# A gated recurrent layer on one core: the products with the state in three banks of 128 columns

## The chip, the core and the metric

The kernel runs on one NeuronCore of a Trainium2 chip. Five engines work beside each other, each through its own instructions in order: TensorE (PE, with the weight loads shown as a row of their own, PEld), VectorE (DVE), ScalarE (ACT), GpSimd (POOL) and SyncE (SP, which issues the DMAs). They meet at semaphores. [...] The metric is the device time of one execution in microseconds; the kernel before takes 1627.62 us in the median of three runs (1627.06 to 1628.18).

## The reference

Eight sequences of 512 steps, 512 features wide, go through one recurrent layer with a gate `r` on the hidden product and an output gate `z`, and the input is added to the result. With `h` the state (8 x 512, float32):

```
fused  = sigmoid([x_t, h] @ w_W + w_b)            # 512+512 wide
r, z   = split(fused)
memory = x_t @ wx_W + wx_b + r * (h @ wh_W + wh_b)
h_new  = z * h + (1 - z) * tanh(memory)
out_t  = x_t + h_new
```

Everything with `x_t` alone can be computed ahead, for many steps at once. The three products with `h` (`r`, `z` and `hh = h @ wh_W`, 512 x 512 each) can't: they stand in a chain of 512 steps.

## The kernel before

**Layout.** The 512 features are cut into four pieces of 128 (`k`, 0 to 3, on the partitions as rows of the contraction) and the 512 outputs into four quarters (`j`) of 32 partitions. Of the outputs there are two halves: half A is what contraction pieces 0 and 1 of the next step need, half B what pieces 2 and 3 need. So `z` of half A is 64 columns on 128 partitions, and likewise `r`, `hh` and half B: six blocks of 64 columns a step.

**The products with the state** (lines 535 to 552). For a piece `k` the state (128 x 32: four steps of eight sequences, of which one step counts) is loaded as the weights, and the columns of the weight matrices stream through. Each product is four matmuls, one for each quarter `j`, which run side by side in the array, and each float32 matmul stands in the trace as two. A *group* here means four such matmuls beside each other: a product of one `k` with one bank is two groups, eight matmul records. `ORDER` says in which order `(bank, k)` come:

- bank A, `k` 0 and 1: 256 columns: the part of `hh` of half B, `hh`, `z` and `r` of half A
- bank A, `k` 2 and 3: 192 columns (without `hh` of half B)
- bank D, `k` 0 to 3: 128 columns, `z` and `r` of half B
- bank H, `k` 2 and 3: 64 columns, the rest of `hh` of half B

`hh` of half B so lies in two pieces, in banks A and H. PSUM is filled ahead with the input's part and the bias (`spread`, ScalarE), four steps at a time, and the two sets of banks alternate every four steps. Behind the state's products of a step come products of the input for later chunks (`deal`, into the banks `xp`), three units of 96 columns in most steps and four in one of sixteen; the last sixteen steps have none. DVE drains them (`drain`, line 431), SP moves halves across partitions and POOL adds up (`result`).

**After the products.** Features must get back onto partitions, so each block is turned by a 32 x 32 transpose on VectorE. VectorE's order in a step is written out by hand (lines 654 to 683): turn `r` of A (`tr`, line 577); turn `hh` of A (`md1A`, 592); turn `z` of A (`tz`, 577); a mark (`settle`, 600: a one-element memset that waits until an earlier transpose has finished writing, since VectorE does not wait for its own results); two scans `m` of half A (`memory`, 565); turn the first part of `hh` of B (`md1B`, 636); turn `r` of B (`tr<-D`); the first update of half A (`update`, 565: a scan `hT<-hd0A`); turn the second part of `hh` of B (592); the second update of A; a mark; two scans `m` of B; two transposes of `z` of B (`hd0B`, 629); a mark (632); two updates of B (`hT<-hd0B`). Then come whatever drains and transposes of the input's part fall due (`turn_x`), and two idle memsets (710). The scans multiply and add along short chains: `m` of B has three terms, of A two.

ScalarE's order is the sigmoid of `r` of A, the sigmoid of `z` of A (both from turned SBUF tiles), two tanh of A, two sigmoids for `r` of B, the sigmoid of `z` of B straight from bank D, two tanh of B, two copies of the new state. Then come the copies of `spread`.

Pieces 0 and 1 of the next step wait for the updates of half A, pieces 2 and 3 for those of half B.

Of the kernel before, what the change touches and what calls it, by code (L numbers as in the profile page):

```python
# [7 lines left out]
F32 = mybir.dt.float32  # L8
BF16 = mybir.dt.bfloat16
AF = mybir.ActivationFunctionType  # L10
# [3 lines left out]
P = 128  # L14
NQ = 4
GS = 4
B = 8
HU = 64
# [3 lines left out]
DVE_FILL = 23  # L22
IDLE = 5
# [34 lines left out]
AHEAD = (  # L58
    (((), ""), ((0,), "AD"), ((1, 2, 3), "H")),
    (((0,), "A"), ((1,), "D"), ((2, 3), "H")),  # L60
    (((0,), "A"), ((1, 2, 3), "D"), ((), "H")),
    (((0,), "A"), ((1, 2), "D"), ((3,), "H")),
)
# [6 lines left out]

SC = slice(128, 512)

XP = {"A": slice(0, 256), "X": slice(256, 384), "D": slice(384, 512), "H": slice(512, 576)}


@with_exitstack
def tile_cond_rnn_residual(
# [111 lines left out]
    nc.scalar.activation(const.tile([P, 1], F32, name="table"), zeros[:, :1], AF.Sigmoid)  # L189
    for n, t_ in enumerate(hd0[0] + hd0[1] + md0[0] + md0[1] + hT[0] + hT[1] + md1[1]):  # L190
        (nc.vector if n < DVE_FILL else nc.gpsimd).memset(t_, 0.0)
    for t_ in md0[1]:
        nc.gpsimd.memset(t_[:, :, :, 1], 1.0)
    for t_ in hd0[0] + hd0[1]:
# [10 lines left out]
    tt = const.tile([P, 7 * BL], F32, name="tt")  # L205
    xs = [const.tile([P, 576], F32, name=f"xs{n}") for n in range(4)]

# [15 lines left out]

    for t_ in xps + [whole[1]["H"], whole[1]["A"]] + list(banks[0].values()):
        mm(t_, none, none[:, :1].broadcast_to([P, t_.shape[1]]), start=True)
    for n in range(2):
        mm(whole[1]["D"], zeros[:, :128], zeros, start=n == 0)

    def bank_of(g):

        return {2: whole[1]["H"], 3: whole[1]["A"], 4: whole[1]["D"]}.get(g, xps[g % 2])

# [24 lines left out]
    for t_ in off:  # L257
        nc.gpsimd.memset(t_, 0.0)
    for t_ in xs:
        nc.gpsimd.memset(t_[:, :64], 0.0)  # L260
    for t_ in xs[1:] + xs[:1]:
        nc.gpsimd.tensor_copy(t_[:, 64:128], bias[:, :64])
        nc.gpsimd.tensor_copy(t_[:, 512:], bias[:, 448:])
    c0 = COLS.start
# [41 lines left out]
    def source(g, c0, c1):  # L306

        return xs[g % GS][:, c0:c1] if g else xps[0][:, c0 - 64 : c1 - 64]

    def spread(g, names):  # L310

        for n in names:
            skip = 64 if n == "A" and not g else 0
            nc.scalar.copy(banks[g % 2][n][:, skip:], source(g, XP[n].start + skip, XP[n].stop))

    def turn_x(g, e):

        c0 = XP["X"].start + 32 * e
        nc.vector.transpose(md1[e // 2][g % 2][:, :, e % 2, 1 + e // 2], source(g, c0, c0 + 32))

# [158 lines left out]
    for n in (2, 1, 3):  # L479
        weight_sum(n, slice(0, 1))  # L480
    spread(0, "HDA")
    keep(1)
# [41 lines left out]
    for i in range(T):  # L524
# [10 lines left out]
        for n in (ORDER if i else FIRST).split():  # L535
            if n == "x":
                take(first[1], 1)
                if k_ == 0:
                    keep(2)
                k_ += 1  # L540
                continue
            bank, k = n[0], int(n[1])
            hs = hT[k // 2][i % NH][:, :, k % 2, 2]
            to, w_ = {
                "A": (ps["A"], wa) if k < 2 else (ps["A"][:, 64:], wa[:, :, :, 64:]),
                "D": (ps["D"], wd),
                "H": (ps["H"], wa[:, :, :, :64]),
            }[bank]
            if bank == "A" and i == 0:
                to, w_ = xps[0][:, :HALF], wa[:, :, :, 64:]  # L550
            for j in range(NQ):
                mm(to[32 * j : 32 * j + 32, :], hs, w_[:, k, j])
# [18 lines left out]

        pa = ps["A"][:, HU:] if i else xps[0][:, :HALF]
        raw = {"h": (pa[:, :HU], ps["H"]), "z": (pa[:, HU : 2 * HU],), "r": (pa[:, 2 * HU :], ps["D"][:, HU:])}

        def turned(n, hf):
            t_ = work.tile([P, 2, 32], F32, tag=f"t{n}{hf}", name=f"t{n}{hf}_{i}")
            inst = nc.vector.transpose(t_.rearrange("p c n -> p (c n)"), raw[n][hf]).ins  # L577
            return t_[:, :, rows], inst

        h_done = [None, None]  # L580

        def turn_r():
            tr, _ = turned("r", 0)
            act(
                ("r", 0, g % 2, s),
                md0[0][g % 2][:, rows, :, 1].rearrange("p n c -> p c n"),
                tr,
                AF.Sigmoid,
            )

        def turn_h(hf):
            inst = nc.vector.transpose(  # L592
                md1[hf][g % 2][:, :, :, hf].rearrange("p n c -> p c n"), raw["h"][hf]
            ).ins
            h_done[hf] = inst
# [3 lines left out]
        def settle(hf):  # L599
            inst = nc.vector.memset(idle[:, IDLE - 2 + hf : IDLE - 1 + hf], 0.0).ins  # L600
            tc.add_manual_dep(inst, h_done[hf].name, SYNC)

        def turn_z():
            tz, _ = turned("z", 0)
            settle(0)
            act(
                ("zc", i % 2),
                hd0[0][i % 2][:, :, :, 2].rearrange("p n c -> p c n"),
                tz,
                AF.Sigmoid,  # L610
                scale=-1.0,
            )

        def turn_r_b():
            t_, _ = turned("r", 1)
            for q in range(2):
                act(
                    ("r", 1, q, g % 2, s),
                    md0[1][g % 2][:, rows, q : q + 1, 2].rearrange("p n c -> p c n"),
                    t_[:, q : q + 1],  # L620
                    AF.Sigmoid,
                )
            sz = work.tile([P, HU], F32, tag="sz", name=f"sz_{i}")
            act(("sz", i % 4), sz, ps["D"][:, :HU], AF.Sigmoid, scale=-1.0)
            return sz

        def turn_sz(sz):
            done = [
                nc.vector.transpose(hd0[1][i % 2][:, :, q, 2], sz[:, 32 * q : 32 * q + 32]).ins  # L629
                for q in range(2)  # L630
            ]
            mark = nc.vector.memset(idle[:, IDLE - 3 : IDLE - 2], 0.0).ins
            tc.add_manual_dep(mark, done[0].name, SYNC)

        def turn_part():
            nc.vector.transpose(md1[1][g % 2][:, :, :, 0].rearrange("p n c -> p c n"), ps["A"][:, :HU])  # L636

        ms = [
            work.tile([P, 2, B, 2 + hf], F32, tag=f"m{hf}", name=f"m{hf}_{i}").rearrange("p c n s -> p n c s")
            for hf in range(2)  # L640
        ]

        def memory(hf, q):

            c_ = slice(q, q + 1)
            scan(c_, ms[hf], md0[hf][g % 2][:, rows], md1[hf][g % 2][:, rows])
            act(("n", hf, q, i % NH), state(hf, i, 1)[:, :, c_], ms[hf][:, :, c_, 1 + hf], AF.Tanh)

        def update(hf, q):
            new = hT[hf][(i + 1) % NH][:, B * s1 : B * s1 + B]  # L650
            z_ = hd0[hf][i % 2][:, rows] if hf else hd0[hf][i % 2]
            return scan(slice(q, q + 1), new, z_, hT[hf][i % NH][:, rows])
# [12 lines left out]
        update(0, 0)  # L665
        turn_h(1)
        update(0, 1)
        settle(1)
        if i == 0:

# [9 lines left out]
        memory(1, 1)  # L680
        turn_sz(sz)
        update(1, 0)
# [10 lines left out]
        if i < 3:  # L693
            spread(1, "HDA"[i])
            turn_x(1, i)
# [11 lines left out]
        for w in late.get(i, ()):  # L707
            inner_weight(*w)
        for n in range(IDLE - 3):
            nc.vector.memset(idle[:, n : n + 1], 0.0)  # L710
# [104 lines left out]
```

## Time and profile before

| | |
|---|---|
| median of three runs | 1627.62 us (1627.06 to 1628.18) |
| span of the profiled execution, first to last instruction | 1625.9 us |
| TensorE matmul rows busy | 1616.3 us (99%) |
| TensorE weight loads busy | 1308.3 us (80%) |
| VectorE busy | 1411.1 us (87%) |
| ScalarE busy | 1023.8 us (63%) |
| GpSimd busy | 539.1 us (33%) |
| granted TensorE clock | 1.000 over the span |

The span is that of the profiled execution alone; the runs' median is 1.7 us above it. Busy times of PE overlap (a matmul's record goes from its start to its modelled end, and the next has long begun), so 99% says that PE always had something in flight, not that it could not be fed faster. How long a stage takes is read from the chain of waits, which cuts PE's time without overlap, and from the starts of the rows in the timeline. One step is some 3.1 us.

### The profile page before, as it was taken

Reading aid. Unit: us, or ns where it says so; the run is one execution under the profiler, and the core shown is the slowest. Engines: PE = TensorE matmul, PEld = TensorE weight load, DVE = VectorE, ACT = ScalarE, POOL = GpSimd, SP = SyncE. Lnnn points to the kernel's source line nnn. Section 1 sums busy time; section 2 is a strip of 40 time slices with the busy share of each in tenths; the row PEclk is TensorE's granted clock in tenths of the full one; section 3 lists DMA queues with packets and bytes.
Section 4 is the critical chain, followed back from the end, with each engine's and each line's share of the span. In section 5 each row is a group of like instructions: output and inputs, shape, how many; then the busy total and the mean of one; then the engine's idle time right before and its main releaser. Section 6 shows DMA issues by size and latency. Waiting matters only on the chain.

```text
span 1625.9 us, 120027 instructions
## 1 busy us (share of the span) xinstructions
PE 1616.3 (99%) x49211; PEld 1308.3 (80%) x49211; DVE 1411.1 (87%) x11757; ACT 1023.8 (63%) x6033; POOL 539.1 (33%) x1443
## 2 busy tenths in 40 slices
PE   9999999999999999999999999999999999999998
PEld 5888888888888888888888888888888888888876
DVE  8988888888888888888888888888888888888887
ACT  4666666666666666666666666666666666666665
POOL 2323333333333333333333333333333333333321
PEclk9999999999999999999999999999999999999999
DMA  4011111111111111111111111111111111110110
GB/s 192 12 40 33 29 37 38 43 32 33 31 43 39 35 34 31 39 38 39 33 29 37 38 43 32 30 35 43 38 33 34 32 39 38 39 34 25 31 35 10
DMA packets 66217, 62.04 MB, mean 38 GB/s; under 512 B 9856, under 2 KB 64000, under 8 KB 65664
## 3 DMA queue, kind: packets, MB, share of 16 engines
q1 hardware_dynamic: 65664, 54.35, 12.7%
q8 instruction: 385, 6.31, 1.7%
q14 instruction: 168, 1.38, 0.3%
HBM read 14.96 MB, written 8.39 MB: 14 GB/s over the span
## 4 chain that ended last, share of the span: by engine, by line
PE 98%; DVE 1%; issue 0%; ACT 0%; DVEq 0%
PE A L219 49%; PE D L219 27%; PE xp L219 16%; PE H L219 7%; DVE tr L577 0%; DVE m L565 0%; DVE md1B L636 0%; DVE hT L565 0%; DVE md1A L592 0%; DVE tz L577 0%; DVE zeros L185 0%; DVE hd0B L629 0%; DVE md1B L592 0%; DVE idle L600 0%; ACT hT L285 0%
## 5 line engine op out<-in xcount | busy, mean ns | idle before, releaser
L219 PE MATMUL A<-wa,hT 128*32 128x256 f32 x16352 | 877.8, 355 | 4.2 <-DVE hT L565 4.2
L219 PEld LDWEIGHTS A<-wa,hT 128*32 128x32 f32 x16352 | 497.5, 123 | 260.2 <-DVE hT L565 135.6
L219 PE MATMUL D<-wd,hT 128*32 128x128 f32 x16384 | 541.0, 273 | 0.0
L219 PEld LDWEIGHTS D<-wd,hT 128*32 128x32 f32 x16384 | 480.4, 122 | 21.8 <-DMA wd<-in_wd_dram 0.5
L731 POOL TENSOR_TENSOR ot<-xin,hT 128x32 f32<-128x32 f32 x503 | 134.4, 267 | 1046.5 <-DVE hT L565 1028.8
L285 ACT ACTIVATE md0A<-tr 128x16 f32<-128x16 f32 x512 | 112.9, 221 | 385.2 <-DVE tr L577 385.2
L285 ACT ACTIVATE hT<-m 128x8 f32<-128x8 f32 x2048 | 324.2, 207 | 46.8 <-DVE m L565 0.4
L577 DVE STREAM_TRANSPOSE tr<-A 128x64 f32<-128x64 f32 x511 | 127.8, 250 | 199.4 <-PE A L219 198.2
L285 ACT ACTIVATE hT<-hT 128x16 f32<-128x16 f32 x1024 | 232.3, 227 | 91.4 <-DVE hT L565 89.9
L219 PE MATMUL H<-wa,hT 128*32 128x64 f32 x8208 | 208.3, 219 | 0.0
L285 ACT ACTIVATE md0B<-tr 128x8 f32<-128x8 f32 x1024 | 160.0, 206 | 42.6 <-DVE tr L577 1.2
L219 PEld LDWEIGHTS H<-wa,hT 128*32 128x32 f32 x8208 | 185.6, 122 | 0.0
L565 DVE TENSOR_TENSOR_SCAN hT<-hd0B,hT 128x24 f32<-128x24 f32 x1024 | 171.4, 208 | 0.8 <-DVE hT L565 0.8
L565 DVE TENSOR_TENSOR_SCAN hT<-hd0A,hT 128x24 f32<-128x24 f32 x1024 | 171.9, 168 | 0.0
L565 DVE TENSOR_TENSOR_SCAN m<-md0B,md1B 128x24 f32<-128x24 f32 x1024 | 154.5, 193 | 0.5 <-issue 0.4
L629 DVE STREAM_TRANSPOSE hd0B<-sz 128x32 f32<-128x32 f32 x1024 | 148.5, 190 | 0.0
L565 DVE TENSOR_TENSOR_SCAN m<-md0A,md1A 128x16 f32<-128x16 f32 x1024 | 142.5, 181 | 5.1
L219 PE MATMUL xp<-ti,si 128*32 128x192 f32 (+1 forms) x3120 | 146.7, 295 | 0.0
L450 POOL TENSOR_TENSOR xs<-ff 128x192 f32<-128x192 f32 x240 | 139.5, 597 | 0.1
L636 DVE STREAM_TRANSPOSE md1B<-A 128x64 f32<-128x64 f32 x511 | 130.1, 255 | 0.0
L285 ACT ACTIVATE hd0A<-tz 128x16 f32<-128x16 f32 x512 | 116.6, 228 | 21.2
L592 DVE STREAM_TRANSPOSE md1B<-H 128x64 f32<-128x64 f32 x512 | 128.3, 251 | 0.0
(110 smaller groups left out, 1861.0 us busy)
## 6 DMA issues: line engine op xcount, KB each, us to landing
ff<-tt SPq DMA_DIRECT2D x120, 96.0 KB, 2.6
ff<-tt SPq DMA_DIRECT2D x120, 72.0 KB, 2.2
out_dram<-ot SPq DMA_DIRECT2D x128, 64.0 KB, 1.8
xin<-in_x_dram SPq DMA_DIRECT2D x112, 64.0 KB, 2.1
ff<-ff SPq DMA_DIRECT2D x60, 96.0 KB, 2.1
ff<-ff SPq DMA_DIRECT2D x60, 72.0 KB, 2.7
wx<-in_wx_dram SPq DMA_DIRECT2D x4, 768.0 KB, 7.3
wa<-in_wa_dram SPq DMA_DIRECT2D x4, 512.0 KB, 11.1
```

What stands on the lines that cost most here:

```text
L219: nc.tensor.matmul(out_, lhsT, rhs, start=start, stop=False, skip_group_check=True)
L285: inst = nc.scalar.activation(out_, in_, func, **kw).ins
L450: nc.gpsimd.tensor_tensor(to, a, b, ALU.add)
L565: return nc.vector.tensor_tensor_scan(*[t_[:, :, c_].rearrange("p n c s -> p (n c s)") for t_ in (out_, d0, d1)], 0.0, ALU.mult, ALU.add,).ins
L577: inst = nc.vector.transpose(t_.rearrange("p c n -> p (c n)"), raw[n][hf]).ins
L592: inst = nc.vector.transpose(md1[hf][g % 2][:, :, :, hf].rearrange("p n c -> p c n"), raw["h"][hf]).ins
L629: nc.vector.transpose(hd0[1][i % 2][:, :, q, 2], sz[:, 32 * q : 32 * q + 32]).ins
L636: nc.vector.transpose(md1[1][g % 2][:, :, :, 0].rearrange("p n c -> p c n"), ps["A"][:, :HU])
L731: pool_done[i + 1] = nc.gpsimd.tensor_tensor(ot[:, t], x_of(c, slice(0, NQ), t, 1), hTs[(i + 1) % NH][:, :, :, B * s1 : B * s1 + B, 2].rea ...
```

## The change

The six blocks of 64 columns are dealt out anew over the three banks, now P, Q and R, 128 columns each and for all four `k`: P holds `hh` and `r` of half A, Q holds `z` of half A and `r` of half B, R holds `z` and `hh` of half B. `hh` of half B is in one piece, so its first part is no longer turned by itself, and the scans `m` of half B have two terms as those of A have. `z` of half A goes through the sigmoid on ScalarE from PSUM (as `z` of half B did before) and is turned by VectorE afterwards, all 64 columns at once, behind the two scans `m` of half A; before, VectorE turned it first and ScalarE worked on the turned tile. `r` of half B takes one sigmoid instead of two. There is one mark more (four). The columns of the input's products, the bias and `xs` are reordered to fit.

The order of the products becomes `P0 P1 Q0 Q1 P2 P3 Q2 Q3 R0 R1 R2 R3`, then the input's units as before.

VectorE's order becomes: turn `r` of A, turn `hh` of A, mark, two scans `m` of A, turn `z` of A (from SBUF), turn `r` of B, mark, two updates of A, turn `hh` of B, mark, two scans `m` of B, two transposes of `z` of B, mark, two updates of B. ScalarE's becomes: sigmoid `r` of A, sigmoid `z` of A, two tanh, sigmoid `r` of B, sigmoid `z` of B, two tanh, two copies.

```diff
-ORDER = "A0 A1 A2 A3 D0 D1 D2 D3 H2 H3"
-FIRST = "A0 A1 x A2 x x A3 H0 H1 H2 H3 x D0 D1 D2 D3"
-BANKS = {"A": 256, "D": 128, "H": 64}
+ORDER = "P0 P1 Q0 Q1 P2 P3 Q2 Q3 R0 R1 R2 R3"
+FIRST = "P0 P1 x P2 x x P3 Q0 Q1 Q2 Q3 x R0 R1 R2 R3"
+BANKS = {"P": 128, "Q": 128, "R": 128}
...
-    md0 = [[pair(n, f"md0{n}{i}", 32, m) for i in range(2)] for n, m in (("A", 2), ("B", 3))]
-    md1 = [[pair(n, f"md1{n}{i}", 32, m) for i in range(2)] for n, m in (("A", 2), ("B", 3))]
-    hd0 = [[pair(n, f"hd0{n}{i}", m, 3) for i in range(2)] for n, m in (("A", B), ("B", 32))]
+    md0 = [[pair(n, f"md0{n}{i}", 32, m) for i in range(2)] for n, m in (("A", 2), ("B", 2))]
+    md1 = [[pair(n, f"md1{n}{i}", 32, m) for i in range(2)] for n, m in (("A", 2), ("B", 2))]
+    hd0 = [[pair(n, f"hd0{n}{i}", m, 3) for i in range(2)] for n, m in (("A", 32), ("B", 32))]
...
-            to, w_ = {
-                "A": (ps["A"], wa) if k < 2 else (ps["A"][:, 64:], wa[:, :, :, 64:]),
-                "D": (ps["D"], wd),
-                "H": (ps["H"], wa[:, :, :, :64]),
-            }[bank]
+            to = ps[bank] if i or bank != "P" else xps[0][:, XP["P"]]
+            w_ = {"P": wa[:, :, :, :128], "Q": wa[:, :, :, 128:], "R": wd}[bank]
...
-        raw = {"h": (pa[:, :HU], ps["H"]), "z": (pa[:, HU : 2 * HU],), "r": (pa[:, 2 * HU :], ps["D"][:, HU:])}
+        raw = {"h": (pa[:, :HU], ps["R"][:, HU:]), "r": (pa[:, HU:], ps["Q"][:, HU:]), "z": (ps["Q"][:, :HU], ps["R"][:, :HU])}
...
+        def gate_z(hf):
+            sz = work.tile([P, HU], F32, tag=f"sz{hf}", name=f"sz{hf}_{i}")
+            act(("sz", hf, i % 4), sz, raw["z"][hf], AF.Sigmoid, scale=-1.0)
             return sz
 
-        def turn_part():
-            nc.vector.transpose(md1[1][g % 2][:, :, :, 0].rearrange("p n c -> p c n"), ps["A"][:, :HU])
+        def turn_z(hf, sz):
+            to = hd0[hf][i % 2][:, :, :, 2].rearrange("p n c -> p c n")
+            if hf == 0:
+                return nc.vector.transpose(to, sz).ins
+            return [nc.vector.transpose(to[:, q], sz[:, 32 * q : 32 * q + 32]).ins for q in range(2)][0]
...
-        turn_r()
-        turn_h(0)
-        turn_z()
+        turn_r(0)
+        done = turn_h(0)
+        sz = gate_z(0)
+        settle(0, done)
         memory(0, 0)
         memory(0, 1)
-        if i:
-            turn_part()
-        else:
+        done = turn_z(0, sz)
+        if i == 0:
             for p in (3, 4):
                 inner_weight(0, p)
-        sz = turn_r_b()
+        turn_r(1)
+        settle(1, done)
         update(0, 0)
-        turn_h(1)
         update(0, 1)
-        settle(1)
+        done = turn_h(1)
+        sz = gate_z(1)
+        settle(2, done)
...
         memory(1, 1)
-        turn_sz(sz)
+        done = turn_z(1, sz)
+        settle(3, done)
         update(1, 0)
         update(1, 1)
```

The rest of the diff is the same rearrangement in the host's packing of the weights and the bias, in the columns of `xs` (512 wide instead of 576, four GpSimd memsets at the start less), and in the names.

More of the change, by code (lines that the diff above doesn't have):

```diff
@@ L69 @@
 COLS = slice(64, 448)
[L71 to L73 removed]
+SC = COLS
+XP = {"P": slice(0, 128), "Q": slice(128, 256), "X": slice(256, 384), "R": slice(384, 512)}
 @with_exitstack
@@ L189, in tile_cond_rnn_residual @@
     nc.scalar.activation(const.tile([P, 1], F32, name="table"), zeros[:, :1], AF.Sigmoid)
-    for n, t_ in enumerate(hd0[0] + hd0[1] + md0[0] + md0[1] + hT[0] + hT[1] + md1[1]):
+    for n, t_ in enumerate(hd0[0] + hd0[1] + md0[0] + md0[1] + hT[0] + hT[1]):
         (nc.vector if n < DVE_FILL else nc.gpsimd).memset(t_, 0.0)
-    for t_ in md0[1]:
-        nc.gpsimd.memset(t_[:, :, :, 1], 1.0)
     for t_ in hd0[0] + hd0[1]:
@@ L205, in tile_cond_rnn_residual @@
     tt = const.tile([P, 7 * BL], F32, name="tt")
-    xs = [const.tile([P, 576], F32, name=f"xs{n}") for n in range(4)]
+    xs = [const.tile([P, 512], F32, name=f"xs{n}") for n in range(4)]
     def state(hf, i, slot=2):
@@ L306, in source @@
     def source(g, c0, c1):
-        return xs[g % GS][:, c0:c1] if g else xps[0][:, c0 - 64 : c1 - 64]
+        return xs[g % GS][:, c0:c1] if g else xps[0][:, c0:c1]
     def spread(g, names):
         for n in names:
-            skip = 64 if n == "A" and not g else 0
-            nc.scalar.copy(banks[g % 2][n][:, skip:], source(g, XP[n].start + skip, XP[n].stop))
+            nc.scalar.copy(banks[g % 2][n], source(g, XP[n].start, XP[n].stop))
     def turn_x(g, e):
         c0 = XP["X"].start + 32 * e
-        nc.vector.transpose(md1[e // 2][g % 2][:, :, e % 2, 1 + e // 2], source(g, c0, c0 + 32))
+        nc.vector.transpose(md1[e // 2][g % 2][:, :, e % 2, 1], source(g, c0, c0 + 32))
     def block(at, k, b, j=slice(0, 2)):
@@ L570, in scan, with settle, turn_r @@
             ).ins
-        pa = ps["A"][:, HU:] if i else xps[0][:, :HALF]
-        raw = {"h": (pa[:, :HU], ps["H"]), "z": (pa[:, HU : 2 * HU],), "r": (pa[:, 2 * HU :], ps["D"][:, HU:])}
[L575 to L583, printed above, removed]
-            act(
-                ("r", 0, g % 2, s),
-                md0[0][g % 2][:, rows, :, 1].rearrange("p n c -> p c n"),
-                tr,
+        pa = ps["P"] if i else xps[0][:, XP["P"]]
+        raw = {"h": (pa[:, :HU], ps["R"][:, HU:]), "r": (pa[:, HU:], ps["Q"][:, HU:]), "z": (ps["Q"][:, :HU], ps["R"][:, :HU])}
+        def settle(n, inst):
+            mark = nc.vector.memset(idle[:, 2 + n : 3 + n], 0.0).ins
+            tc.add_manual_dep(mark, inst.name, SYNC)
+        def turn_r(hf):
+            t_ = work.tile([P, 2, 32], F32, tag=f"tr{hf}", name=f"tr{hf}_{i}")
+            nc.vector.transpose(t_.rearrange("p c n -> p (c n)"), raw["r"][hf])
+            act(
+                ("r", hf, g % 2, s),
+                md0[hf][g % 2][:, rows, :, 1].rearrange("p n c -> p c n"),
+                t_[:, :, rows],
                 AF.Sigmoid,
@@ L603, in turn_z @@
[L603 to L624, printed above, removed]
-            return sz
@@ L627, in turn_sz @@
[L627 to L633, printed above, removed]
-        def turn_part():
-            nc.vector.transpose(md1[1][g % 2][:, :, :, 0].rearrange("p n c -> p c n"), ps["A"][:, :HU])
+            return inst
+        def gate_z(hf):
+            sz = work.tile([P, HU], F32, tag=f"sz{hf}", name=f"sz{hf}_{i}")
+            act(("sz", hf, i % 4), sz, raw["z"][hf], AF.Sigmoid, scale=-1.0)
+            return sz
@@ L638, in tile_cond_rnn_residual @@
+        def turn_z(hf, sz):
[3 more added lines that the diff above has]
+            return [nc.vector.transpose(to[:, q], sz[:, 32 * q : 32 * q + 32]).ins for q in range(2)][0]
         ms = [
-            work.tile([P, 2, B, 2 + hf], F32, tag=f"m{hf}", name=f"m{hf}_{i}").rearrange("p c n s -> p n c s")
+            work.tile([P, 2, B, 2], F32, tag=f"m{hf}", name=f"m{hf}_{i}").rearrange("p c n s -> p n c s")
@@ L708, in tile_cond_rnn_residual @@
             inner_weight(*w)
-        for n in range(IDLE - 3):
+        for n in range(2):
             nc.vector.memset(idle[:, n : n + 1], 0.0)
@@ L789 @@
     bias_d = (
-        cat((whb, half_a), (zb, half_a), (rb, half_a), (wxb, both), (zb, half_b), (rb, half_b), (whb, half_b))[0]
+        cat((whb, half_a), (rb, half_a), (zb, half_a), (rb, half_b), (wxb, both), (zb, half_b), (whb, half_b))[0]
     )
```

45 lines of the change are left out of this document (18 added, 27 removed).

## The prediction

> **What bounds the kernel now.** I read the chain of waits first, over the long even middle of the span, then the count of instructions that turns its shares into a time for one step, then who waits for whom.
>
> ```profile
> by line: PE A L219 49.0%; PE D L219 27.9%; PE xp L219 16.0%; PE H L219 7.1%
> ```
> ```profile
> L219 PE MATMUL D<-wd,hT 128*32 128x128 f32 x8192 | 270.5, 273 | 0.0
> ```
> ```profile
> PEld A L219 <- DVE hT L565: 135.6, 499, 0.8
> ```
> ```profile
> L577 DVE STREAM_TRANSPOSE tr<-A x511: 239/250/254, 24.6 to 1621.0; 128x64 f32<-128x64 f32 x171
> ```
>
> The first two rows are the chain and the group of bank D between 400 and 1200 us. The chain is all TensorE. D issues 32 matmul records a step, so 8192 are 256 steps, and the shares of 800 us give for one step A 1.531, D 0.872, H 0.222 and the input's xp 0.500 us, 3.125 together. The last row gives the mean step of the run: (1621.0 - 24.6) / 510 = 3.130 us.
>
> That the chain is all PE does not yet say that PE's own pace is the limit. D takes 8 groups (four matmuls beside each other), 0.109 us each for 128 columns; H takes 4 groups, 0.0555 each for 64. That is 0.836 ns a column and 2.0 ns a group. By this A, four groups of 256 and four of 192 columns, should take 1792 x 0.836 ns + 8 x 2.0 ns = 1.514 us. It takes 1.531: 0.017 us a step is missing. The third row shows where: 499 times in 512 steps the weight load of A waits for a state update. The loads run ahead, so little of that wait reaches the matmuls; but the kernel stands at a balance, and the recurrence is 0.017 us the longer of two nearly equal loops. One step of the chain, and VectorE in it:
>
> ```profile
> 801.38 0.87 PE D L219 x32
> 802.26 0.22 PE H L219 x16
> 802.48 0.49 PE xp L219 x16
> 802.97 1.54 PE A L219 x32
> ```
> ```profile
> 801.45 0.25 DVE L577 STREAM_TRANSPOSE tr<-A 128x64 f32<-128x64 f32 x1 [0.51 <-PE A L219]
> ...
> 801.99 0.28 DVE L565 TENSOR_TENSOR_SCAN m<-md0A,md1A 128x16 f32<-128x16 f32 x2
> 802.19 0.25 DVE L636 STREAM_TRANSPOSE md1B<-A 128x64 f32<-128x64 f32 x1
> 802.34 0.24 DVE L577 STREAM_TRANSPOSE tr<-D 128x64 f32<-128x64 f32 x1
> 802.50 0.17 DVE L565 TENSOR_TENSOR_SCAN hT<-hd0A,hT 128x24 f32<-128x24 f32 x1
> 802.59 0.26 DVE L592 STREAM_TRANSPOSE md1B<-H 128x64 f32<-128x64 f32 x1
> 802.74 0.17 DVE L565 TENSOR_TENSOR_SCAN hT<-hd0A,hT 128x24 f32<-128x24 f32 x1
> 802.89 0.20 DVE L565 TENSOR_TENSOR_SCAN m<-md0B,md1B 128x24 f32<-128x24 f32 x1
> 802.91 0.06 DVE L600 MEMSET idle<- 128x1 f32 x1
> 803.01 0.18 DVE L565 TENSOR_TENSOR_SCAN m<-md0B,md1B 128x24 f32<-128x24 f32 x1
> 803.11 0.29 DVE L629 STREAM_TRANSPOSE hd0B<-sz 128x32 f32<-128x32 f32 x2
> 803.37 0.06 DVE L632 MEMSET idle<- 128x1 f32 x1
> 803.37 0.33 DVE L565 TENSOR_TENSOR_SCAN hT<-hd0B,hT 128x24 f32<-128x24 f32 x2
> 803.63 0.56 DVE L431 TENSOR_TENSOR tt<-xp,ee 128x384 f32<-128x384 f32 x1
> 804.11 0.20 DVE L319 STREAM_TRANSPOSE md1A<-xs 128x32 f32<-128x32 f32 x1
> 804.26 0.07 DVE L710 MEMSET idle<- 128x1 f32 x2
> 804.58 0.25 DVE L577 STREAM_TRANSPOSE tr<-A 128x64 f32<-128x64 f32 x1 [0.25 <-PE A L219]
> ```
> ```profile
> 803.63 0.34 PEld L219 LDWEIGHTS A<-wa,hT 128*32 128x32 f32 x12 [0.27 <-DVE hT L565]
> ```
>
> Follow the loop. A ends at 801.38; VectorE starts 0.07 later and works without a break to the first update of half B at 803.37, 1.99 us after A's end. From there 0.26 us to the load of piece 2, and 0.88 from the load to the next end of A (802.97 + 1.54 = 804.51). The sum is 3.13 us, a hair more than PE's own 1.514 + 0.872 + 0.222 + 0.49 = 3.10. The last steps, which have no input products to fill PE, confirm it:
>
> ```profile
> 1602.38 0.25 DVE tr L577
> ...
> 1621.05 0.25 DVE tr L577
> ```
>
> These are six steps apart: 3.112 us a step with PE a sixth of the time out of work. Shorten this loop and at most 0.017 us a step comes back; lengthen it and every bit is paid.
>
> **The change, part by part.**
>
> *TensorE.* Columns stay: 2 x 256 + 2 x 192 + 4 x 128 + 2 x 64 = 1536 before, 12 x 128 = 1536 after. Groups go from 20 to 24 a step, with 16 matmuls and 16 loads more. At D's pace the state's products take 24 x 0.109 = 2.616 us, and nothing hides that, since PE is full. Before they took 1.531 + 0.872 + 0.222 = 2.625 with the stall. If the stall goes entirely: -0.009 us a step, made of -0.017 for the stall and +0.008 for four groups. Input products, SP's and GpSimd's transfers in a step are untouched; four GpSimd memsets and narrower `xs` at the start lie beside PE's input passes and are put at nothing.
>
> [...]
>
> *VectorE and ScalarE, half A.* P is complete after `P2 P3`: four groups of 128 behind the late state instead of four of 192, so 0.21 us earlier counted from the update of B. The `r`, `hh` and scans of A keep their spacing (turn to `m`: 801.45 to 801.99, 0.54). `z` of A leaves the place ahead of the scans, where VectorE had idle time, and stands behind them, in the place of the first part of `hh` of B. No row shows a 64-column transpose out of SBUF. The nearest are the 0.15 from the part's start to the next instruction (802.19 to 802.34) above and, below, half of a pair of 32-column ones, 0.11. I take 0.15. ScalarE's sigmoid of 64 columns for it needs Q, which ends 0.44 after P; with 0.07 to start, 0.20 (`sz` below) and 0.03 it is done 0.74 after P's end, and the transpose's turn comes at 0.07 + 0.54 + 0.20 = 0.81, so it is hidden. The second mark waits for that transpose; its own 0.06 us may or may not count.
>
> *Half B.* Here is the new critical path: `hh` and `z` of B both stand in R, the last bank. From the update of B: 0.26 to the load; 0.88 - 4 x 0.163 + 4 x 0.109 = 0.67 to the end of P (0.163 for 192 columns, from xp's 576 in 0.49); Q's and R's remaining 12 groups, 1.31; R ends 2.24 us after the update. Then three ways lead to the next update, whose pieces before are:
>
> ```profile
> 802.22 0.31 ACT L285 ACTIVATE hT<-m 128x8 f32<-128x8 f32 x2
> 802.61 0.31 ACT L285 ACTIVATE md0B<-tr 128x8 f32<-128x8 f32 x2
> 802.83 0.20 ACT L285 ACTIVATE sz<-D 128x64 f32<-128x64 f32 x1
> 803.12 0.32 ACT L285 ACTIVATE hT<-m 128x8 f32<-128x8 f32 x2
> ```
> ```profile
> DVE md1A L319 <- ACT A L314: 0.5, 1, 0.5
> ```
>
> VectorE's own: 0.07 to the turn of `hh`, 0.30 to the first `m` (802.59 to 802.89), 0.11 to the second, 0.09 to the transposes of `z` (the spacing behind two-term scans at 801.99), 0.26 to the update: 0.83. By tanh: 0.07 + 0.30 + 0.23 (802.89 to 803.12) + 0.25 to the update (803.12 to 803.37) = 0.85. By `z`: the last row shows VectorE waiting at the start for a ScalarE copy although both only read one bank, so I expect the sigmoid of `z` to wait until VectorE has turned `hh` out of R: 0.07 + 0.25 + 0.03 (802.58 to 802.61) + 0.20 + 0.03 + 0.26 = 0.84. The loop is 2.24 + 0.85 = 3.09 us, 0.03 shorter than before; PE's 2.616 + 0.49 = 3.11 us is longer. So the stall goes and PE's pace decides.
>
> [...]
>
> *What is late next.* VectorE must be free when R ends, 1.31 us after P's end. From the turn of `r` of A: 0.54 to `m`, 0.20 to `z`, 0.15, 0.16 for `r` of B (802.34 to 802.50), the mark 0 to 0.06, two updates of A at 0.09 (802.50 to 802.59): free at 1.23 to 1.29. If these updates space as B's do, since their `hd0` tile now has B's layout, 0.12 apiece (first two rows below), 1.29 to 1.35. I take 1.26, by A's own rows.
>
> ```profile
> 52.20 0.21 DVE L565 TENSOR_TENSOR_SCAN hT<-hd0B,hT 128x24 f32<-128x24 f32 x1
> 52.20 0.06 DVE L632 MEMSET idle<- 128x1 f32 x1
> 52.32 0.21 DVE L565 TENSOR_TENSOR_SCAN hT<-hd0B,hT 128x24 f32<-128x24 f32 x1
> ...
> 53.36 0.07 DVE L710 MEMSET idle<- 128x1 f32 x2
> ```
>
> The window for drains between B's update and the turn of `r` shrinks from 1.21 us (803.37 to 804.58) to 0.26 + 0.67 + 0.07 = 1.00. The step shown needs 0.89 (803.37 to 804.26), one of the fuller, so the drains still fit. The first sixteen steps carry VectorE's preparation of weights, 1.16 us in the step of the last fence: some 0.1 to 0.2 us too much in about half of them, together +1.0 us (0.5 to 1.5).
>
> *The sum.* Some 480 middle steps at -0.009: -4.3 us. Sixteen last ones, bound by the loop, at about -0.02: -0.3. The early ones +1.0. Together -3.6 us on the profiled execution's own span of 1625.9, so 1622.3; the runs' median lies 1.7 us above that span, and 1627.62 - 3.6 = 1624.0 us.
>
> **The rivals.**
>
> *VectorE comes late to `hh` of B.* Place: the turn of `r` of B, the mark and two updates of A now all stand between A's scans and the turn out of R. For it: the bound of 1.35, 0.04 beyond R. Against it: A's updates at 0.09. It decides from a lateness of 0.02 (PE's 3.11 is passed); at 0.03 the kernel is no faster. At 0.05 the loop is 3.14, +0.02 on 3.12: 496 x 0.02 = +10, about 1638 us. [...]
>
> *About no change.* R's path is 0.02 to 0.03 longer than summed (a wait more at ScalarE ahead of the sigmoid of R, a slower turn), and the loop is 3.12 again: 1627.6 us. For it: three ways of nearly one length, each added to hundredths. Against: two-term scans make `m` shorter, never longer.
>
> *The 0.017 is not the wait.* If A's gap came from going over to narrower products, the four groups would cost +0.008 x 496 = +4: 1631.6 us, plus the early steps. Against: the last steps show the loop's length without PE.
>
> *Weight loads become the bound*, the change then doing the reverse of its purpose: if loads of 0.122 us could not overlap, 24 x (0.122 - 0.109) = +0.31 a step, 1786 us. D's pace denies it.
>
> **How the numbers follow.** PE's pace decides: 0.50, with a range of its own of 1621.8 to 1625.5. No change: 0.22. VectorE late: 0.21. Not the wait: 0.05. Loads: 0.02. About 0.2%, 3.3 us, is what can be told from no change here. The forecast's 0.50 lies across that line: 0.39 faster, 0.11 within it. Adding 0.05 of the no-change case that ends a little below, faster has 0.44; within 0.11 + 0.15 = 0.26; slower the rest, 0.30. The range goes from 1621.5, the forecast with no cost in the early steps, to 1638, VectorE late by 0.05.
>
> **What would show it.** Right: in the chain of the middle stretch P, Q and R take 0.87 us each; the loads' wait for the state loses its share in the matmuls; the turn of `hh` of B starts 0.07 after R's end; the last steps come 3.09 apart. Wrong: VectorE still in an update of A when R ends; a gap in P between pieces 1 and 2; the sigmoid of `z` of B starting well after the turn of `hh`; steps of 3.13 or more.

## The result, and the profile after

The changed kernel takes 1701.59 us in the median (1700.80 to 1708.84), beside 1627.34 us (1626.75 to 1628.18) of the kernel before, measured with it: a ratio of 1.0465, 95% interval 1.0445 to 1.0484. It is 74 us slower. The prediction said 1624.0, in a range from 1621.5 to 1638.0: wrong in its sign and by far more than its range.

The head of the page after, the span and the busy times:

```profile
span 1699.8 us, 135865 instructions
...
PE 1680.6 (99%) x57387; PEld 1590.4 (94%) x57387; DVE 1484.7 (87%) x11758; ACT 994.4 (58%) x5521; POOL 538.3 (32%) x1435
```

The turn of `r` of A once more gives the mean step (tile `tr` after; shortest, median and longest duration, first and last start):

```profile
L571 DVE STREAM_TRANSPOSE tr<-P x511: 236/250/253, 25.1 to 1694.7; 128x64 f32<-128x64 f32 x171
```

(1694.7 - 25.1) / 510 = 3.274 us, 0.144 more than before; 510 times that is 73 us, the whole loss. It is spread over the steps. Chain of waits, 400 to 1200 us, and the group of bank R there:

```profile
by line: PE P L217 28.0%; PE Q L217 27.8%; PE R L217 27.2%; PE xp L217 15.3%; issue 0.9%; DVE m L555 0.2%; DVE hT L555 0.2%; DVE tr L571 0.1%; DVE hd0B L596 0.1%; ACT md0A L281 0.1%; DVE md1B L580 0.1%; DVE hd0A L595 0.1%; ACT sz L281 0.0%
```
```profile
L217 PE MATMUL R<-wd,hT x7808: 269/273/316, 400.3 to 1198.8; 128*32 128x128 f32 x196
```

7808 records are 244 steps of 32. P takes 0.918 us a step, Q 0.911, R 0.892, where 0.87 each was forecast; the input's products take 0.502, as before. No row of another engine in the chain is over 0.2%. What has come in is "issue", time in which TensorE waited for nothing that the profile shows. Waits after (total us, times, longest):

```profile
DVE tr L571 <- PE P L217: 92.5, 292, 0.9
ACT hT L281 <- DVE m L555: 33.4, 145, 0.4
...
DVE md1B L580 <- PE R L217: 15.3, 44, 0.7
PEld R L217 <- issue: 15.0, 50, 0.7
PEld Q L217 <- issue: 14.3, 51, 0.5
PEld P L217 <- DVE hT L555: 13.1, 46, 0.5
PEld xp L217 <- issue: 13.0, 43, 1.5
...
PEld P L217 <- issue: 8.4, 30, 0.7
```

and before:

```profile
PEld xp L219 <- issue: 2.5, 13, 0.2
...
PEld A L219 <- issue: 1.7, 9, 0.2
...
PEld D L219 <- issue: 1.3, 4, 0.5
...
PEld H L219 <- issue: 1.2, 6, 0.2
```

The loads' wait for the state has fallen from 135.6 us to 13.1: that stall did go. In its place the loads stand still for 50.7 us (8.4 + 14.3 + 15.0 + 13.0) with no releaser; before it was 6.7. The timeline after shows what that does:

```profile
801.51 0.12 PEld L217 LDWEIGHTS xp<-ti,so 128*32 128x32 f32 x3
801.53 0.14 PEld L217 LDWEIGHTS R<-wd,hT 128*32 128x32 f32 x1
...
801.57 0.36 PE L217 MATMUL xp<-ti,so 128*32 128x192 f32 x3
...
801.65 0.27 PE L217 MATMUL R<-wd,hT 128*32 128x128 f32 x1
...
805.52 0.11 PEld L217 LDWEIGHTS xp<-ti,xin 128*32 128x32 f32 x1 [0.26 <-issue]
```

At 801.65 the last matmul of R starts on one quarter of the array when three quarters have begun the input's products 0.08 earlier: the four streams no longer go in step. Between 400 and 1200 us the input's products begin ahead of the last matmul of the state in 38% of the steps; in the kernel before, they do so in none. At 805.52 the loads had stood for 0.26 us with no wait to account for it. That speaks for instructions that reach TensorE late.

The page counts how they come. Busy times and DMA queues (packets, MB, share of the engines' time) before, and the queue after:

```profile
PE 1616.3 (99%) x49211; PEld 1308.3 (80%) x49211; DVE 1411.1 (87%) x11757; ACT 1023.8 (63%) x6033; POOL 539.1 (33%) x1443
...
q8 instruction: 385, 6.31, 1.7%
```
```profile
q8 instruction: 448, 7.34, 1.9%
```

6.31 MB / 385 and 7.34 MB / 448 are 16,384 bytes a packet. TensorE's records, matmuls and loads together, are 2 x 49211 before and 2 x 57387 after: 256 for each packet in both. So the instructions of TensorE come in blocks of 256, and a step needs 192 of them before and 224 after. A block lasts 3.130 x 256 / 192 = 4.17 us before and 3.274 x 256 / 224 = 3.74 us after. If a block can't come faster than in about 3.74 us, a step of 224 instructions can't take less than 3.27 us, whatever the products cost.

The trace keeps the time of each of these packets. After, one starts every 3.74 us in the mean, takes 1.14, and the next starts 2.60 after its end, at the soonest 2.29; before, the three means are 4.17, 1.12 and 3.04. Loads of Q, R or `xp` start more than 0.25 us after the load ahead of them 125 times (the first and last 60 us left out); in the kernel before, loads of D, H or `xp` never do. Each of the 125 pauses ends 1.20 to 1.68 us after the end of a packet, at all places of the step; counted in instructions, all end within one stretch of some 90 in every 256. The pause that ends at 805.52 is one of them: the packet ended at 804.06. So the pauses go with the blocks, not with a place in the step. Nor is it that TensorE takes instructions no faster: in the kernel before, bank H's 16 matmuls and 16 loads take 0.222 us, a pace at which 256 would take 1.8.

### The profile page after: what moved, and what is told of

The parts are those of the page before. It is cut to its first block, busy times and chain, and to the rows that moved or that the text cites. A ratio compares the mean times of both kernels' runs of the same rounds, so it can differ in the third digit from the quotient of the medians.

```text
span 1699.8 us, 135865 instructions
## 1 busy us (share of the span) xinstructions
PE 1680.6 (99%) x57387; PEld 1590.4 (94%) x57387; DVE 1484.7 (87%) x11758; ACT 994.4 (58%) x5521; POOL 538.3 (32%) x1435
## 3 DMA queue, kind: packets, MB, share of 16 engines
q8 instruction: 448, 7.34, 1.9%
q14 instruction: 165, 1.34, 0.3%
## 4 chain that ended last, share of the span: by engine, by line
PE 97%; DVE 1%; issue 1%; ACT 0%; ACTq 0%
PE P L217 28%; PE Q L217 27%; PE R L217 26%; PE xp L217 15%; DVE m L555 0%; DVE tr L571 0%; DVE hT L555 0%; ACT md0A L281 0%; DVE hd0A L595 0%; DVE hd0B L596 0%; DVE md1B L580 0%; ACT sz L281 0%; ACT hT L281 0%; DVE ti L333 0%; DVE zeros L185 0%
## 5 line engine op out<-in xcount | busy, mean ns | idle before, releaser
L217 PE MATMUL P<-wa,hT 128*32 128x128 f32 x16352 | 715.3, 276 | 4.4 <-issue 1.7
L217 PE MATMUL Q<-wa,hT 128*32 128x128 f32 x16384 | 712.5, 273 | 2.8 <-issue 1.4
L217 PE MATMUL R<-wd,hT 128*32 128x128 f32 x16384 | 586.6, 273 | 4.5 <-issue 3.1
L217 PEld LDWEIGHTS Q<-wa,hT 128*32 128x32 f32 x16384 | 545.2, 122 | 15.1 <-issue 12.8
L217 PEld LDWEIGHTS P<-wa,hT 128*32 128x32 f32 x16352 | 508.0, 123 | 43.0 <-DVE hT L555 13.1
L217 PEld LDWEIGHTS R<-wd,hT 128*32 128x32 f32 x16384 | 496.1, 122 | 17.0 <-issue 13.8
L281 ACT ACTIVATE hT<-m 128x8 f32<-128x8 f32 x2048 | 321.3, 206 | 65.7 <-DVE m L555 33.4
L571 DVE STREAM_TRANSPOSE tr<-P 128x64 f32<-128x64 f32 x511 | 127.6, 250 | 105.3 <-PE P L217 92.5
L555 DVE TENSOR_TENSOR_SCAN m<-md0B,md1B 128x16 f32<-128x16 f32 x1024 | 139.3, 178 | 21.9
L580 DVE STREAM_TRANSPOSE md1B<-R 128x64 f32<-128x64 f32 x512 | 125.9, 246 | 16.9 <-PE R L217 15.3
L595 DVE STREAM_TRANSPOSE hd0A<-sz 128x64 f32<-128x64 f32 x512 | 129.5, 253 | 7.1 <-ACT sz L281 6.3
```

Source lines behind the costliest of these rows:

```text
L217: nc.tensor.matmul(out_, lhsT, rhs, start=start, stop=False, skip_group_check=True)
L281: inst = nc.scalar.activation(out_, in_, func, **kw).ins
L555: return nc.vector.tensor_tensor_scan(*[t_[:, :, c_].rearrange("p n c s -> p (n c s)") for t_ in (out_, d0, d1)], 0.0, ALU.mult, ALU.add,).ins
L571: nc.vector.transpose(t_.rearrange("p c n -> p (c n)"), raw["r"][hf])
L580: inst = nc.vector.transpose(md1[hf][g % 2][:, :, :, 0].rearrange("p n c -> p c n"), raw["h"][hf]).ins
L595: return nc.vector.transpose(to, sz).ins
```

## The experiments

Theory 1 throughout: the supply of TensorE's instructions sets the step, at about 3.74 us for 256, wherever that is longer than the step's other limits. The rivals are numbered within each expectation.

**The kernel before with more instructions and the same columns.** Three kernels cut products of bank A into a part of 128 columns and the rest: pieces 2 and 3 (224 instructions a step), all four pieces (256), piece 2 alone (208). Order, columns and every other engine's work stay.

```diff
-            for j in range(NQ):
-                mm(to[32 * j : 32 * j + 32, :], hs, w_[:, k, j])
+            cuts = ((0, 128), (128, w_.shape[3])) if bank == "A" and i and k in (2, 3) else ((0, w_.shape[3]),)
+            for c0_, c1_ in cuts:
+                for j in range(NQ):
+                    mm(to[32 * j : 32 * j + 32, c0_:c1_], hs, w_[:, k, j, c0_:c1_])
```

> The kernel before, with the 192-column products of bank A (pieces 2 and 3) cut into 128 and 64 columns: same columns, same VectorE and ScalarE work, but 224 PE instructions (matmuls and loads) a step instead of 192, as many as in the changed kernel. Theory 1 (TensorE is not supplied with instructions fast enough: in the changed kernel 256 instructions take 3.74 us at the median): 224/256 x 3.74 = 3.27 us a step, about 1700 us. Theory 2 (groups of 128 columns are slow because of their weight loads; 16 more of them cost 74 us in the changed kernel): four more groups of 128 and four of 64, at most +37, about 1650 to 1665 us. Theory 3 (VectorE's scans are held up by GpSimd): nothing but the 8 ns of four groups, 1627 to 1633 us.

> As the run before, and the 256-column products of pieces 0 and 1 cut into 128 and 128 as well: 256 PE instructions a step. Theory 1: 256/256 x 3.74 us a step, about 1930 us. Theory 2: twelve more groups of 128 and four of 64, less than the changed kernel's 1702 us or about that. Theory 3: 1627 to 1640 us.

> The kernel before with only the 192-column product of piece 2 cut into 128 and 64: 208 PE instructions a step. Theory 1: 208/256 x 3.74 = 3.04 us, under the step's 3.12, so a loss only where single blocks of instructions come late (3.4 to 4.2 us are seen for one): 1629 to 1645 us. If the law were simply proportional to the instructions beyond 192: half of the 77 us of 224, about 1665 us.

224 instructions: 1705.24 us, ratio 1.048 (1.0455 to 1.0504), the loss of the changed kernel without any of its change. 256: 1949.21 us, 1.199 (1.1961 to 1.2019). 208: 1635.54 us, 1.0049 (1.0034 to 1.0064). Tile `tr`, first with 224, then with 256, then with 208:

```profile
L579 DVE STREAM_TRANSPOSE tr<-A x511: 236/250/253, 25.8 to 1695.5; 128x64 f32<-128x64 f32 x171
```
```profile
L579 DVE STREAM_TRANSPOSE tr<-A x511: 240/250/253, 24.6 to 1951.6; 128x64 f32<-128x64 f32 x171
```
```profile
L579 DVE STREAM_TRANSPOSE tr<-A x511: 238/250/253, 25.3 to 1626.7; 128x64 f32<-128x64 f32 x171
```

The steps are 3.274, 3.778 and 3.140 us. In blocks of 256 that is 3.74, 3.78 and 3.86 us. (The execution profiled with 256 was the slowest of its four, 0.5% above the median.) The first 16 instructions more cost 0.010 us a step, the next 16 0.134, the next 32 0.504. It is a threshold and then nearly a straight line through the origin, not a price for each instruction. With 256 the wait is plain (waits):

```profile
PEld A L219 <- issue: 262.1, 463, 1.2
```

At 4.17 us a block, in the kernel before, the loads' waits at "issue" are 6.7 us in all; at 3.74, with two products cut, they are 53.0 (D 19.2, `xp` 14.7, A 10.1, H 9.0).

**The changed kernel with fewer instructions, first form.** Q0 and Q1 stream 256 columns, R0 and R1 are left out; the columns stay, the instructions are 192 a step. A twin leaves GpSimd's additions of the result out as well.

```diff
+            if bank == "R" and i and k in (0, 1):
+                continue
+            if bank == "Q" and i and k in (0, 1):
+                w2 = wa.rearrange("p k j c -> p (k j c)")
+                for j in range(NQ):
+                    c_ = (k * NQ + j) * 256 + 128
+                    mm(whole[g % 2]["Q"][32 * j : 32 * j + 32, :256], hs, w2[:, c_ : c_ + 256])
+                continue
```

> The changed kernel with 192 PE instructions a step and the same columns: the products of Q with pieces 0 and 1 are 256 columns wide (the second half is thrown away), the products of R with pieces 0 and 1 are left out, so half B's z and hh lack these two pieces. VectorE, ScalarE and GpSimd do the same as in the changed kernel. Theory 1: the step falls back to PE's pace of 3.10 or the loop's 3.11, 1622 to 1640 us (the upper end if VectorE is held up by GpSimd in a third of the steps as well). Theory 2: eight more groups of 128 than before, 1655 to 1670 us. Theory 3: unchanged, about 1700 us.

> As the run before, and GpSimd's additions of the Strassen results (the 192-column ones into ff and xs) are left out, so the input's part is wrong as well. Theory 1: 1620 to 1627 us, the difference to the run before being what GpSimd's holding up of VectorE's scans costs (0.145 us in 153 steps, of which 0.07 reach the loop: about 11 us). Theory 2: as the run before, 1655 to 1670 us. Theory 3: about 1625 us, while the run before stays at 1700 us.

1723.07 us (ratio 1.059, 1.0574 to 1.0605) and 1722.95 us (1.0588, 1.057 to 1.0606): every theory missed. The waits and the timeline of the first say why:

```profile
PEld P L217 <- DVE hT L563: 142.6, 507, 0.8
...
PEld xp L217 <- issue: 4.1, 19, 0.8
```
```profile
800.86 0.25 DVE L579 STREAM_TRANSPOSE tr<-P 128x64 f32<-128x64 f32 x1 [0.31 <-PE P L217]
...
802.00 0.18 DVE L563 TENSOR_TENSOR_SCAN hT<-hd0A,hT 128x24 f32<-128x24 f32 x1
...
802.13 0.66 PE L217 MATMUL P<-wa,hT 128*32 128x128 f32 x16
...
802.61 1.05 PE L217 MATMUL Q<-wa,hT 128*32 128x256 f32 x16
...
803.47 0.62 PE L217 MATMUL P<-wa,hT 128*32 128x128 f32 x16
...
804.16 0.25 DVE L579 STREAM_TRANSPOSE tr<-P 128x64 f32<-128x64 f32 x1 [0.33 <-PE P L217]
```

The waits at "issue" are nearly gone, as theory 1 has it, but the edit made a new loop. From the update of half A to the start of P2, P0, P1 and the wide Q0 and Q1 now take 802.13 to 803.47 = 1.34 us; with 1.14 from turn to update, 0.13 to the load and 0.69 from P2 to the next turn the loop over half A is 3.30 us, against the step of (1715.9 - 24.9) / 510 = 3.316. The pair says nothing on the supply. It says that columns put between the pieces of the early and of the late state lengthen a loop, and it says what form the next pair needs: the wide products last.

**Second form.** R0 and R1 stream 256 columns, R2 and R3 are left out; again 192 instructions, the same columns, and nothing moved ahead of the late state. Again a twin has no GpSimd additions.

```diff
+            if bank == "R" and i and k in (2, 3):
+                continue
+            if bank == "R" and i and k in (0, 1):
+                w2 = wd.rearrange("p k j c -> p (k j c)")
+                for j in range(NQ):
+                    c_ = (k * NQ + j) * 128
+                    mm(whole[g % 2]["R"][32 * j : 32 * j + 32, :256], hs, w2[:, c_ : c_ + 256])
+                continue
```
```diff
-                at_step(w0 + w + m, *[(result, e, n) for n in todo])
+                pass
```

> The changed kernel with 192 PE instructions a step, the columns ahead of the late state left as they are: the products of R with pieces 0 and 1 are 256 columns wide (the second half is thrown away), those of R with pieces 2 and 3 are left out, so half B's z and hh lack these pieces. R ends at the same point of the step. In the run with wide products of Q the extra columns stood ahead of the late state, and the loop over half A became the limit; here they don't. Theory 1 (instruction supply): no waits put down to issue, step 3.11 to 3.15 us, 1622 to 1640 us. Theory 2 (weight loads of 128-column groups, eight more than before): 1655 to 1670 us. Theory 3 (GpSimd holds up VectorE): about 1700 us.

> As the run before, without GpSimd's additions of the Strassen results (192 columns, into ff and xs; the input's part is then wrong as well). Theory 1 with a second, smaller cause: 1620 to 1627 us, up to 11 us below the run before; if GpSimd costs nothing here, the same as the run before.

1637.59 us (ratio 1.0061, 1.0046 to 1.0076) and 1628.4 us (1.0006, 0.9996 to 1.0015). 64 of the 74 us are gone with 32 instructions a step; the remaining 9.2 go with GpSimd's additions. The groups of the scan `m` of half A (busy us, mean ns, idle before), first of the one, then of the other:

```profile
L563 DVE TENSOR_TENSOR_SCAN m<-md0A,md1A 128x16 f32<-128x16 f32 x1024 | 169.0, 205 | 14.4
```
```profile
L563 DVE TENSOR_TENSOR_SCAN m<-md0A,md1A 128x16 f32<-128x16 f32 x1024 | 141.7, 180 | 14.3
```

169.0 - 141.7 = 27 us of scans: a second cause, smaller, which the prediction had not named. In the changed kernel it stands in the timeline:

```profile
800.18 1.15 POOL L445 TENSOR_TENSOR ff<-ff 128x192 f32<-128x192 f32 x2
...
801.05 0.41 DVE L555 TENSOR_TENSOR_SCAN m<-md0A,md1A 128x16 f32<-128x16 f32 x2
```

and in the kernel before it doesn't (groups):

```profile
L565 DVE TENSOR_TENSOR_SCAN m<-md0A,md1A 128x16 f32<-128x16 f32 x1024 | 142.5, 181 | 5.1
```

The pair of scans takes 0.41 us instead of 0.28 when GpSimd's additions still run (to 801.33 here), and ScalarE's tanh waits for such scans 145 times in the waits after, 33.4 us. The A stage begins some 0.2 us sooner after the update of B than before, as the prediction had it, and so meets the same additions earlier in their course. The trace shows the two tied together: in the changed kernel 158 scans start with more than 0.15 us of an addition still to run, and each ends 0.04 to 0.05 us after that addition; in the kernel before there are three. By what means the addition holds the scan up is not shown.

1628.4 us is what the change has to give when both costs are away: no gain. (The second form has also four groups less, 20 for 24, and leaves two products out, so it is near the change and not the change itself.)

**208 instructions, and the transfers.** One kernel has R0 wide and R2 left out (208 instructions); another is the changed kernel without the DMAs that move the drained halves, in case the blocks come late because of other transfers.

```diff
-        if q in (6, 4):
-            nc.sync.dma_start(out=ff[e][here, own], in_=to[here])
-        if q in (1, 6, 7, 4):
-            nc.sync.dma_start(out=ff[e][here, moved], in_=to[there])
```

> The changed kernel with one product of a step less: R0 streams 256 columns (128 of them junk into columns that nobody reads) and R2 is left out, so the output is not the reference's; the same columns stream, with 208 TensorE instructions a step instead of 224. Theory 1 (step = the longer of TensorE's pace and n/256 x 3.74 us): 208 gives 3.04 us, under the pace of 3.11, so the supply lets go: the time of the 192-instruction form (1637.6) plus at most the 8 us that 208 instructions cost the kernel before, 1636 to 1648 us. Theory 3 (each instruction more has its price): halfway between 1637.6 and 1701.6, about 1669.

> The changed kernel without the 360 DMAs that move halves of the drained results across partitions (so the input's part is wrong; the buffers are zeroed at the start). Instructions are fetched by DMA as well: if the other transfers slow the fetches, a block comes sooner (0.9 instead of 1.1 us of transfer), 224/256 x 3.5 = 3.06 us a step, and the kernel falls to 1630 to 1660 us; if a fetch takes its time whatever else is moved, 1695 to 1702 us.

With 208 instructions: 1642.3 us, ratio 1.009 (1.0075 to 1.0105), within theory 1's bounds. Sixteen instructions out of 224 are worth 59 us. Without the transfers: 1700.32 us, ratio 1.0443 (1.0412 to 1.0474), no different from the changed kernel; these transfers don't set the pace of the blocks.

**The changed kernel without GpSimd's additions**, 224 instructions, the edit of the twins alone.

> The changed kernel with its 224 TensorE instructions a step, but GpSimd's 192-column additions of the result are left out (so the output is not the reference's). Theory 1 (the supply of TensorE's instructions, 256 in about 3.74 us, sets the step at 224/256 x 3.74 = 3.27 us, and the scan that GpSimd holds up lies hidden behind it): 1696 to 1702 us, although the same omission took 9.2 us off the 192-instruction form. Theory 2 (the two costs add up): 9 us less than the changed kernel, about 1692.

1722.25 us (1718.01 to 1727.31), ratio 1.0572 (1.0551 to 1.0594): 21 us slower than the changed kernel, where nothing or a gain of 9 was expected: both theories missed. Its waits, its tile `tr` and its scans:

```profile
PEld Q L217 <- issue: 22.8, 66, 0.7
PEld R L217 <- issue: 22.2, 69, 0.7
...
PEld P L217 <- issue: 15.5, 52, 0.7
...
PEld xp L217 <- issue: 10.7, 42, 0.7
```
```profile
L571 DVE STREAM_TRANSPOSE tr<-P x511: 239/250/252, 24.9 to 1720.4; 128x64 f32<-128x64 f32 x171
```
```profile
L555 DVE TENSOR_TENSOR_SCAN m<-md0A,md1A 128x16 f32<-128x16 f32 x1024 | 142.2, 181 | 13.7
```

The scans run undisturbed, and yet the loads stand still for 71.2 us instead of 50.7 at "issue"; a step is 3.325 us, a block 3.80. So undisturbed scans gave no gain here, where the supply binds; but the time of a block isn't a constant either. It was 3.74, 3.74, 3.78 and 3.80 us in four kernels that it bound (the last from the slowest of four executions; their median would give some 3.79). The packets took no longer than in the changed kernel (1.13 us in the mean, 1.14 there); what grew is the time from a packet's end to the next one's start, from 2.60 to 2.67. Whether leaving out GpSimd's additions did it is not shown. This run is from another chip (15) than the cut kernels with 224 and 256 (0) and the one without transfers (8), and no other kernel that the supply binds ran there. The twelve executions of the other three kernels with 224 lie between 1696.4 and 1709.4 us and these four above them all, but a difference between chips is not ruled out.

The steps together, all from tile `tr`, (last start - first start) / 510:

| kernel | TensorE instructions a step | step, us | block of 256, us |
|---|---|---|---|
| before | 192 | 3.130 | 4.17 |
| changed, second form, no additions | 192 | 3.130 | 4.17 |
| changed, second form | 192 | 3.149 | 4.20 |
| before, one product cut | 208 | 3.140 | 3.86 |
| changed, R0 wide | 208 | 3.155 | 3.88 |
| before, two products cut | 224 | 3.274 | 3.74 |
| changed | 224 | 3.274 | 3.74 |
| changed, no additions | 224 | 3.325 | 3.80 |
| before, four products cut | 256 | 3.778 | 3.78 |

(The last sixteen steps have 32 instructions less, so the blocks are a per cent or less longer than the last column has them.) None of these kernels is faster than the kernel before.

## Why the prediction was wrong

**The step that failed** is the sum under *TensorE*: "At D's pace the state's products take 24 x 0.109 = 2.616 us, and nothing hides that". D's pace was read off eight groups in a row, in a kernel whose step as a whole drew 192 instructions in 3.13 us; it says what the array can do with instructions at hand. The same paragraph counted "16 matmuls and 16 loads more" and charged them 2 ns a group, 0.008 us a step. They cost 0.144. Sixteen matmuls and sixteen loads more in the kernel before, without the change, cost the same 0.144. The prediction weighed a limit on loads, and rightly found it not to be one; the supply of instructions was no term of its sum and none of its rivals. The row for it was in the page before: 385 packets of instructions, one every 4.22 us of the span. It gave no limit, but it asked what happens at 24 x 8 + 32 = 224 a step.

**The stall of 0.017 us goes**: the loads' wait for the state is 13.1 us instead of 135.6, and 16.2 in the second form without additions. But the 0.009 us a step that was to come of it did not: that form, which has neither of the two costs, takes 3.130 us a step, as the kernel before. What holds it there no run separates; the loop, next, is longer than forecast. The last steps, at 192 instructions, have the loop alone (timeline after):

```profile
1685.31 0.25 DVE L571 STREAM_TRANSPOSE tr<-P 128x64 f32<-128x64 f32 x1 [0.50 <-PE P L217]
...
1686.49 0.18 DVE L555 TENSOR_TENSOR_SCAN hT<-hd0A,hT 128x24 f32<-128x24 f32 x1
1686.62 0.26 DVE L580 STREAM_TRANSPOSE md1B<-R 128x64 f32<-128x64 f32 x1
...
1687.49 0.20 DVE L555 TENSOR_TENSOR_SCAN hT<-hd0B,hT 128x24 f32<-128x24 f32 x1
...
1688.47 0.25 DVE L571 STREAM_TRANSPOSE tr<-P 128x64 f32<-128x64 f32 x1 [0.60 <-PE P L217]
...
1689.78 0.26 DVE L580 STREAM_TRANSPOSE md1B<-R 128x64 f32<-128x64 f32 x1
...
1690.60 0.20 DVE L555 TENSOR_TENSOR_SCAN hT<-hd0B,hT 128x24 f32<-128x24 f32 x1
...
1691.58 0.25 DVE L571 STREAM_TRANSPOSE tr<-P 128x64 f32<-128x64 f32 x1 [0.61 <-PE P L217]
```

**The loop of half B**: two of its three terms were right within 0.02 us, the third was 0.04 to 0.09 too short. From turn of P to turn of `hh` of B 1.31 (forecast 1.31); from there to the update 0.87 in one step and 0.82 in the next (0.78, the 0.85 less the 0.07 ahead of the turn); from the update to the next turn of P 0.98 (1.00). The loop is 3.16 and 3.11 instead of 3.09, so it is no shorter than PE's 3.11, where the forecast had it 0.02 shorter.

**VectorE late to `hh` of B**: in these steps the turn starts 1.31 behind the turn of P, where R's end was put, and straight behind the second update of A: the two come together, inside the bound of 1.29 to 1.35 that the prediction had for VectorE, and there is no lateness to speak of. Where R is late, VectorE waits for it, 44 times and 15.3 us in the waits after. **The drains fit**: VectorE still stood idle for P 292 times, 92.5 us in all. What VectorE did pay for the earlier A stage was the meeting with GpSimd's additions, which the prediction had left out: it took VectorE's durations from places where nothing stood in their way. VectorE starts an instruction before the one ahead of it has ended (the turn at 1686.62 begins 0.05 us before the end of the update begun at 1686.49); what a step would do without its marks no run here shows.

**`z` of A from SBUF** and **the order of two readers of R** (groups and waits after):

```profile
L595 DVE STREAM_TRANSPOSE hd0A<-sz 128x64 f32<-128x64 f32 x512 | 129.5, 253 | 7.1 <-ACT sz L281 6.3
```
```profile
ACT sz L281 <- DVE md1B L580: 143.8, 511, 1.0
```

The transpose out of SBUF takes 253 ns; the one of `r` out of P takes 250 in the median. The next instruction starts 0.15 us after the start of the transpose of `z` (timeline after, 801.39 to 801.54; the median of all steps is the same), as the prediction took it. The sigmoid of `z` of B waited for the turn of `hh` of B in 511 steps of 512, as the prediction took it too. The wait is for a semaphore, so the trace shows that the program keeps the two readers apart. What two readers at once would do, no run here shows.

**About no change** is the rival that the runs speak for once the two costs are away: the second form without additions is at 1.0006 of the time before. As far as that form stands for the change, the change had nothing to give even with the instructions and the additions out of the way.

## What to carry to other kernels

Count TensorE's instructions in a step, matmuls and loads, and divide by the time of the step: here 256 in 4.17 us were free, 256 in 3.86 nearly so, and no kernel here went below 256 in about 3.74 to 3.80 in the mean. Splitting columns into narrower products spends that supply: with the same 1536 columns and 224 instructions instead of 192, the kernel before took 1705.24 us, 1.048 of its time. A wait of the weight loads with no releaser ("issue", 50.7 us in the changed kernel) and quarters that drift apart (in 38% of its steps between 400 and 1200 us) are how it showed. Moving a stage earlier also moved it against work of an engine that isn't in the chain (a pair of scans took 0.41 us instead of 0.28): ask which of GpSimd's instructions run at the new place before taking VectorE's durations over.

## What the hardware showed that was not expected

- A supply of instructions that binds: blocks of 16,384 bytes, 256 instructions of TensorE, one in 3.74 to 3.80 us at the fastest that a kernel here kept up. At 224 and 256 instructions a step the time follows their number (3.274 and 3.778 us), at 192 and 208 it hardly does (3.130 and 3.140).
- That time was not lowered by taking 360 other DMAs away (1700.32 against 1701.59 us), and was 3.80 instead of 3.74 us a block in the one kernel without GpSimd's additions, on another chip. A packet takes 1.14 us of it; what sets the rest is open.
- Two scans of VectorE, 0.28 us undisturbed, took 0.41 beside a GpSimd addition of 192 columns.
- PEld busy for 94% of the span was no sign that loads were the bound: the kernel before with two products cut took as long (1705.24 us) with PEld busy for 84%, and with 8 loads and 8 matmuls less a step (208 instructions) the changed kernel's columns ran in 59 us less.
